# Two 1024x1024 layers of the last three token blocks, computed as seven products of quarters

## The chip, the core and the metric

The kernel runs on one core of a Trainium2 chip. The metric is the device time of one execution in microseconds (us); a smaller number is better. The engines of a core that matter here are TensorE (PE; its loads of stationary operands are listed apart as PEld), VectorE (DVE), ScalarE (ACT), GpSimd (POOL) and SyncE (SP, which only issues transfers here). POOL issues transfers too.

## What is computed

The input x is 4 x 1024 tokens of width 256. Three steps follow each other, each with a residual: a feed-forward network on normalised tokens (half of it is added), a long convolution over the sequence with a dense layer behind it, and the same feed-forward network again.

```python
h = silu(x @ w1.T * s1) * (x @ w2.T * s2)        # 256 -> 1024, twice
h = gelu(h @ h1.T * s_h1)                        # 1024 -> 1024, "layer 2"
h = gelu(h @ h2.T * s_h2)                        # 1024 -> 1024, "layer 3"
return h @ w3.T * s3                             # 1024 -> 256
```

The weights w1, w2, h1, h2 and w3 are drawn from -1, 0 and 1 (as float32 numbers).

## The kernel before

**Blocks.** The 4096 tokens are cut into eight blocks of 512 (`TB`). The outer loop (line 1029) runs over sixteen turns: f0 to f7 for the first network, g0 to g7 for the second. Between them the convolution ("mix") of each of the four sequences is worked in, and so is the preparation of its kernel.

**Precision.** The matmuls of the network take float32 operands in a reduced format, `float32r`. An activation is split into two such parts: the high part is a converting copy on ACT (line 367 or 379), the low part is the difference to it, made on DVE by `low_part` (line 285, its instruction has line 287). `linear` (line 340) adds up the product with both parts in one PSUM bank, so each weight tile is multiplied with two moving operands of 128x512. The weights are exact in one part, because they are small whole numbers; if they are not, the whole function is run a second time in plain float32 (`macaron_kernel`, line 1049), which does not happen with these inputs. `weight_checks` (line 455) finds that out: it loads each weight piece again in 44 pieces of 128x512 (tile `given`) and compares it on DVE with the resident copy.

**One turn.** `ffn` (line 352) makes 8 pairs of banks pa and pb (64 matmuls, with ACT's Silu and DVE's product behind them), then layer 2 with the resident `h1_sb` and layer 3 with `h2_sb` (8 banks of 16 matmuls each, line 374, with Gelu on ACT at line 377), then the last layer: `last_squares` (line 391, 2 banks of 16 matmuls of 512 columns) or, in turn g7, `last_tokens` (line 410), where activations are the stationary operand and w3 with 256 columns is the moving one (line 423). `xr` is the residual's input, `y` the result.

**Order of the work.** After each of the eight banks of a layer, `ffn` calls `ahead()` and `tick()`. `ahead` pushes `prepare` (line 956) of the next turn by a step: load of x, norm, transposition through a DRAM tile `moved` (POOL stores, line 317, and loads, line 325). `tick` (line 1007) hands out side work (`aside`: convolution and its kernel) for a budget of `STEP_WORK` = 2500, in which an operation on DVE counts its columns and `OP_WORK` = 130. When the side work pauses and more than eight entries are done, it takes a weight check instead. A scheduler of the framework then orders the instructions of each engine; each engine works its own list in order, and waits for others by semaphores. Tiles come from rings: `half` (19 buffers of 128x512), `ring` (15 operand tiles of two parts), and eight PSUM banks.

Of the kernel before, what the change touches and what calls it, by code (L numbers as in the profile page):

```python
# [2 lines left out]

# [8 lines left out]
F32 = mybir.dt.float32  # L12
# [3 lines left out]
ALU = mybir.AluOpType  # L16
# [16 lines left out]
N_WARM = 9  # L33


STEP_WORK, OP_WORK, MIN_WORK = 2500, 130, 300
PAUSE = "pause"
N_CHECKS = 44

EPS = 1e-5  # L40
INV_2PI = 1.0 / (2.0 * math.pi)
# [56 lines left out]
def macaron_layers(  # L98
# [20 lines left out]

    nc = tc.nc
    split = bad is not None
    wide = F32R if split else F32
# [3 lines left out]
    small = ctx.enter_context(tc.tile_pool(name="small", bufs=2))  # L128
    dram = ctx.enter_context(tc.tile_pool(name="dram", bufs=1, space=bass.MemoryType.DRAM))
    psum = ctx.enter_context(tc.tile_pool(name="psum", bufs=8, space=bass.MemoryType.PSUM))  # L130

    work_done = 0

# [18 lines left out]
    def half(name, *shape, dtype=F32):  # L152

        return work.tile([P, *(shape or (512,))], dtype, tag="half", name=name, bufs=19)
# [10 lines left out]
    make_identity(nc, ident)  # L165
    w1_sb = keep.tile([P, DC, HID], wide, name="w1_sb")
    w2_sb = keep.tile([P, DC, HID], wide, name="w2_sb")
    h1_sb = keep.tile([P, KH, HID], wide, name="h1_sb")
    h2_sb = keep.tile([P, KH, HID], wide, name="h2_sb")
    w3_sb = keep.tile([P, KH, D], wide, name="w3_sb")  # L170
    wt_sb = keep.tile([P, DC, D], F32, name="wt_sb")
    w3s_sb = keep.tile([P, D], F32, name="w3s_sb")
# [7 lines left out]

    moved = dram.tile([DC, P, JT, P], F32, name="moved")
    k_hat = dram.tile([2 + len(PAIRS), 2, P, 2, D], F32, name="k_hat")

    def column(i):
        return cst_sb[:, i : i + 1]
# [41 lines left out]
    x_first = work.tile([P, JT, D], F32, tag="xb", name="x_f0", bufs=3)  # L227
    for i, queue in ((0, nc.sync), (2, nc.scalar)):
        queue.dma_start(x_first[:, i : i + 2, :], tokens(x, 0, i, 2))
    eps = small.tile([P, 1], F32, name="eps", bufs=1)  # L230
    nc.vector.memset(eps, EPS)

    unused = small.tile([P, 1], F32, name="unused", bufs=1)
# [115 lines left out]
                    stop=(k == n - 1 and part == parts - 1),  # L349
                )  # L350

    def ffn(xt, src, dst, blk, name, tick, ahead, final):


        ha = []
        for m in range(KH):
            pa, pb = bank(f"pa_{name}_{m}"), bank(f"pb_{name}_{m}")
            linear(pa, w1_sb, m, xt)
            linear(pb, w2_sb, m, xt)
            g = half(f"g_{name}_{m}")  # L360
            t = ring(f"ha_{name}_{m}", parts, TB, dtype=wide)
            nc.scalar.activation(g, pa, AF.Silu, scale=sc_sb[:, 0, m : m + 1])
            nc.vector.scalar_tensor_tensor(  # L363
                g if split else t[:, 0, :], pb, sc_sb[:, 1, m : m + 1], g, ALU.mult, ALU.mult
            )
            if split:
                nc.scalar.copy(t[:, 0, :], g)
                low_part(t, g)
            ha.append(t)
        for layer, w in ((2, h1_sb), (3, h2_sb)):  # L370
            hb = []
            for m in range(KH):
                ps = bank(f"p{layer}_{name}_{m}")
                linear(ps, w, m, ha)
                t = ring(f"h{layer}_{name}_{m}", parts, TB, dtype=wide)
                g = half(f"g{layer}_{name}_{m}") if split else t[:, 0, :]
                nc.scalar.activation(g, ps, AF.Gelu, scale=sc_sb[:, layer, m : m + 1])  # L377
                if split:
                    nc.scalar.copy(t[:, 0, :], g)  # L379
                    low_part(t, g)  # L380
                hb.append(t)
                ahead()
                if layer == 2 or m < KH - 1:
                    tick()
            ha = hb
        ahead(last=True)
        if name == "f0":
            nc.scalar.mul(w3s_half, w3s_half, 0.5)
        (last_tokens if final else last_squares)(ha, src, dst, blk, name)

    def last_squares(ha, src, dst, blk, name):


        rest = []
        for k in range(DC):
            xr = half(f"xr_{name}_{k}", TB // SQ, SQ)
            for c in range(P // SQ):
                nc.sync.dma_start(xr[c * SQ : (c + 1) * SQ], in_squares(src, blk, k, c))
            rest.append(xr)
        for k in range(DC):  # L400
            ps = bank(f"po_{name}_{k}")
            linear(ps, w3_sb, k, ha)
            o, y = half(f"o_{name}_{k}"), half(f"y_{name}_{k}", TB // SQ, SQ)
            nc.scalar.activation(o, ps, AF.Identity, scale=w3s_half[:, k : k + 1])
            nc.vector.transpose(y, o.rearrange("p (n s) -> p n s", s=SQ))
            nc.gpsimd.tensor_tensor(y, rest[k], y, ALU.add)
            for c in range(P // SQ):
                stores.dma_start(in_squares(dst, blk, k, c), y[c * SQ : (c + 1) * SQ])

    def last_tokens(ha, src, dst, blk, name):  # L410

        rest = []
        for i in range(0, JT, 2):
            xr = half(f"xr_{name}_{i}", 2, D)
            nc.sync.dma_start(xr, tokens(src, blk, i, 2))
            rest.append(xr)

        def result(ps, i, n):

            for e in range(n):  # L420
                for k in range(KH):
                    for part in range(parts):
                        nc.tensor.matmul(  # L423
                            ps[:, e * D : (e + 1) * D],
                            ha[k][:, part, (i + e) * P : (i + e + 1) * P],
                            w3_sb[:, k, :],
                            start=(k == 0 and part == 0),
                            stop=(k == KH - 1 and part == parts - 1),
                        )

        def finish(ps, y, xr, i, n, add_on):
            nc.vector.scalar_tensor_tensor(
                y,
                ps.rearrange("p (e d) -> p e d", e=n),
                0.5,
                w3s_sb[:, None, :].to_broadcast([P, n, D]),
                ALU.mult,
                ALU.mult,
            )
            add_on.tensor_tensor(y, xr, y, ALU.add)  # L440
            nc.sync.dma_start(tokens(dst, blk, i, n), y)

        y = half(f"y_{name}_0", 2, D)
        ps = bank(f"po_{name}_0")
        result(ps, 0, 2)
        finish(ps, y, rest[0], 0, 2, nc.gpsimd)
        y = half(f"y_{name}_2", 2, D)
        for e in range(2):
            ps = bank(f"po_{name}_{2 + e}")
            result(ps, 2 + e, 1)  # L450
            finish(
                ps[:, 0:D], y[:, e : e + 1, :], rest[1][:, e : e + 1, :], 2 + e, 1, nc.vector
            )

    def weight_checks():

        todo = []
        for src, held in ((w1, w1_sb), (w2, w2_sb), (h1, h1_sb), (h2, h2_sb), (w3, w3_sb)):
            n_k, width = held.shape[1], held.shape[2]
            by = max(1, 512 // width)  # L460
            for k in range(0, n_k, by):
                for c in range(0, width, 512):
                    cols = slice(c, min(c + 512, width))
                    todo.append((rows(src)[:, k : k + by, cols], held[:, k : k + by, cols]))
        assert len(todo) == N_CHECKS

        def load(n):
            given = half(f"given_{n}", *todo[n][1].shape[1:])
            nc.sync.dma_start(given, todo[n][0])
            return given  # L470

# [2 lines left out]
        for n, (src, held) in enumerate(todo):  # L474
            given = following
            if n + 1 < len(todo):
                following = load(n + 1)
            stt(
                given,
                given,  # L480
                0.0,
                held.bitcast(F32),
                ALU.add,
                ALU.not_equal,
                accum_out=miss[:, n : n + 1],
            )
            yield
# [513 lines left out]

    aside = all_aside()
    checks = weight_checks() if split else iter(())
    ticks = 0
    allowed = 0

    def tick():

        nonlocal ticks, allowed, work_done
        ticks += 1  # L1010
        allowed = min(allowed, work_done) + STEP_WORK
        while work_done < allowed:
            at = work_done
            if next(aside, PAUSE) is PAUSE:
                if len(done) > 8 and allowed - work_done > OP_WORK + TB:
                    next(checks, None)
                break
            if work_done == at:
                work_done += MIN_WORK
# [9 lines left out]
    for n, (turn, blk) in enumerate(blocks):  # L1029
# [3 lines left out]
        def ahead(last=False):  # L1033
            for step in steps:
                if last:
                    done.append(("last layer", *blocks[n + 1][::-1]))
                next(step, None)

        src, dst = (x, x1) if turn == "f" else (x2, out)
        with tc.issue_after(last_split.ins) if n == 0 else nullcontext():  # L1040
            ffn(xt, src, dst, blk, f"{turn}{blk}", tick, ahead, n + 1 == len(blocks))
        done.append((turn, blk))
        xt = following
    for rest in (aside, checks):
        for _ in rest:
            pass


def macaron_kernel(tc: tile.TileContext, *args):
# [72 lines left out]
```

## Time and profile before

| what | value |
|---|---|
| median of 3 runs | 1405.83 us (1405.32 to 1405.91) |
| the profiled execution's own time | 1405.23 us |
| its span in the trace, first to last instruction | 1403.3 us |
| PE busy | 1393.0 us (99%) |
| PEld busy | 1161.4 us (83%) |
| DVE busy | 838.6 us (60%), 1614 instructions |
| ACT busy | 707.6 us (50%), 1070 instructions |
| POOL busy | 266.3 us (19%) |
| DMA | 101.27 MB, mean 72 GB/s |
| granted TensorE clock, mean | 0.999 of full speed |

A group row of the profile reads: line, engine, operation, out<-in, shapes, xcount, then busy time of the group, mean length of one instruction in ns, and the idle time of the engine just ahead of it. Matmuls overlap each other in the records, so their mean length is longer than the distance between two of them; distances are taken from the length of a run of them. A row of the stretches by window gives, for each engine, its busy time in the stretch and in brackets its instructions. Turn g5 runs from 1142 to 1236 us, g6 from 1236 to 1316 us, g7 from 1316 us to the end.

### The profile page before, as it was taken

The page shows a single profiled execution, that of the slowest core. Times are in us where ns is not written, and L with a number is a line of the kernel's source. Part 1 is how long each engine was busy: PE and PEld are TensorE (multiplying, and loading weights), DVE is VectorE, ACT ScalarE, POOL GpSimd, SP SyncE. Part 2 cuts the span into 40 slices and gives each one's busy share as a digit, 9 for nine tenths or more (in the row PEclk, how much of TensorE's full clock was granted, in tenths as well). Part 3 has the DMA queues.
Part 4 walks back from the last instruction along what each step waited for, and adds up shares of the span by engine and source line. Part 5 has one row for each costly group of instructions (what it writes and reads, how often), then busy time and mean ns, then how long its engine had stood idle before and what let it go on. Part 6 is the DMA issues. An engine that isn't in the chain of part 4 may idle for free.

```text
span 1403.3 us, 17882 instructions
## 1 busy us (share of the span) xinstructions
PE 1393.0 (99%) x6492; PEld 1161.4 (83%) x6492; DVE 838.6 (60%) x1614; ACT 707.6 (50%) x1070; POOL 266.3 (19%) x398
## 2 busy tenths in 40 slices
PE   8999999999999999999999999999999999999998
PEld 7888888888888888888888888888888888888887
DVE  6896567755547774387773568753566762542412
ACT  5986579644546344354352454533545342553532
POOL 4321012211312120320113201213112121121200
PEclk9999999999999999999999999999999999999999
DMA  9410101112231322422213404132223122511000
GB/s 355 117 20 26 35 16 46 30 48 77 67 96 30 113 71 73 136 60 84 61 53 113 113 31 138 20 97 74 86 70 82 43 63 98 135 22 39 15 16 19
DMA packets 111139, 101.27 MB, mean 72 GB/s; under 512 B 72304, under 2 KB 82544, under 8 KB 111040
## 3 DMA queue, kind: packets, MB, share of 16 engines
q1 hardware_dynamic: 93248, 55.37, 14.6%
q0 software_dynamic: 17520, 44.39, 11.1%
q8 instruction: 53, 0.87, 0.3%
q14 instruction: 46, 0.38, 0.1%
q10 hardware_dynamic: 272, 0.26, 0.1%
HBM read 76.91 MB, written 23.07 MB: 71 GB/s over the span
## 4 chain that ended last, share of the span: by engine, by line
PE 99%; DMA 1%; POOL 0%; DVE 0%; issue 0%; POOLq 0%
PE p_f L344 33%; PE p_g L344 33%; PE po_f L344 4%; PE pa_g L344 4%; PE pb_g L344 4%; PE pa_f L344 4%; PE pb_f L344 4%; PE po_g L344 4%; PE pi L905 2%; PE pf_m L727 2%; PE pw L930 2%; PE pk L654 1%; PE po_g L423 1%; DMA w_sb<-in_w_dram 1%; PE pf_k L727 0%; POOL w_sb L238 0%
## 5 line engine op out<-in xcount | busy, mean ns | idle before, releaser
L287 DVE TENSOR_TENSOR h_g<-g_g,h_g 128x512 fp32r<-128x512 f32 x128 | 88.6, 692 | 249.6 <-ACT h_g L379 249.3
L344 PE MATMUL p_f<-h_f,h_sb 128*128 128x512 f32 x1024 | 237.1, 391 | 0.0
L344 PE MATMUL p_g<-ha_g,h_sb 128*128 128x512 f32 x1024 | 236.2, 390 | 0.0
L344 PE MATMUL p_f<-ha_f,h_sb 128*128 128x512 f32 x1024 | 235.3, 390 | 0.0
L344 PE MATMUL p_g<-h_g,h_sb 128*128 128x512 f32 x1024 | 235.2, 390 | 0.0
L377 ACT ACTIVATE g_g<-p_g,sc_sb 128x512 f32<-128x512 f32 x128 | 88.2, 689 | 278.9 <-PE p_g L344 276.5
L344 PEld LDWEIGHTS p_g<-ha_g,h_sb 128*128 128x128 f32 x1024 | 192.1, 188 | 39.8
L344 PEld LDWEIGHTS p_g<-h_g,h_sb 128*128 128x128 f32 x1024 | 192.1, 188 | 39.8
L344 PEld LDWEIGHTS p_f<-h_f,h_sb 128*128 128x128 f32 x1024 | 191.8, 188 | 40.1 <-DVE h_f L287 0.3
L344 PEld LDWEIGHTS p_f<-ha_f,h_sb 128*128 128x128 f32 x1024 | 191.9, 188 | 39.8
L377 ACT ACTIVATE g_f<-p_f,sc_sb 128x512 f32<-128x512 f32 x128 | 87.7, 689 | 190.0 <-PE p_f L344 189.6
L287 DVE TENSOR_TENSOR h_f<-g_f,h_f 128x512 fp32r<-128x512 f32 x128 | 87.8, 690 | 149.0 <-ACT h_f L379 148.5
L317 POOL DMA_DIRECT2D moved<-sq_g x64 | 34.9, 552 | 330.3 <-DVE sq_g L140 290.7
L379 ACT CAST h_g<-g_g 128x512 fp32r<-128x512 f32 x128 | 79.3, 620 | 4.0
L379 ACT CAST h_f<-g_f 128x512 fp32r<-128x512 f32 x128 | 78.3, 618 | 2.9
L377 ACT ACT_TABLE_LOAD x51 | 65.4, 1283 | 26.0 <-PE p_f L344 14.3
L344 PE MATMUL pa_f<-xt_f,w_sb 128*128 128x512 f32 x256 | 69.0, 390 | 1.1 <-DVE xt_f L299 0.7
L344 PE MATMUL pb_f<-xt_f,w_sb 128*128 128x512 f32 x256 | 68.8, 389 | 0.0
L344 PE MATMUL pa_g<-xt_g,w_sb 128*128 128x512 f32 x256 | 68.4, 389 | 0.0
L344 PE MATMUL pb_g<-xt_g,w_sb 128*128 128x512 f32 x256 | 68.4, 389 | 0.0
L363 DVE SCALAR_TENSOR_TENSOR g_g<-pb_g,sc_sb,g_g 128x512 f32<-128x512 f32 x64 | 47.9, 749 | 31.5 <-PE pb_g L344 19.7
L317 POOL DMA_DIRECT2D moved<-sq_f x56 | 30.8, 556 | 181.2 <-DVE sq_f L140 181.2
(234 smaller groups left out, 1844.4 us busy)
## 6 DMA issues: line engine op xcount, KB each, us to landing
h_sb<-in_h_dram POOLq DMA_DIRECT2D x8, 1024.0 KB, 15.0
given<-in_h_dram SPq DMA_DIRECT2D x32, 256.0 KB, 3.6
kr<-k_hat SPq DMA_DIRECT2D x20, 256.0 KB, 2.6
ki<-k_hat SPq DMA_DIRECT2D x20, 256.0 KB, 2.8
xr_f<-in_x_dram SPq DMA_DIRECT2D x64, 64.0 KB, 2.4
x<-y_f POOLq DMA_DIRECT2D x64, 64.0 KB, 2.2
xm<-x SPq DMA_DIRECT2D x8, 512.0 KB, 3.7
m_m<-in_cosm_dram SPq DMA_DIRECT2D x16, 256.0 KB, 5.2
```

The costliest lines, as they stand in the source:

```text
L287: return nc.vector.tensor_tensor(t[:, 1, :], src, t[:, 0, :].bitcast(F32), ALU.subtract)
L317: stores.dma_start(moved[k].rearrange("(c r) a q -> a r c q", r=SQ)[a], sq[a * SQ : (a + 1) * SQ].rearrange("r c j s -> r c (j s)"),)
L344: nc.tensor.matmul(ps, w[:, k, m * P : (m + 1) * P], acts[k][:, part, :], start=(k == 0 and part == 0), stop=(k == n - 1 and part == parts ...
L363: nc.vector.scalar_tensor_tensor(g if split else t[:, 0, :], pb, sc_sb[:, 1, m : m + 1], g, ALU.mult, ALU.mult)
L377: nc.scalar.activation(g, ps, AF.Gelu, scale=sc_sb[:, layer, m : m + 1])
L379: nc.scalar.copy(t[:, 0, :], g)
L423: nc.tensor.matmul(ps[:, e * D : (e + 1) * D], ha[k][:, part, (i + e) * P : (i + e + 1) * P], w3_sb[:, k, :], start=(k == 0 and part == 0) ...
L654: nc.tensor.matmul(pk[0:NA, at + i, :, :].rearrange("p h b -> p (h b)"), a[:, i].rearrange("p a b -> p (a b)"), qd[d1 // per_tile][:, at + ...
L727: nc.tensor.matmul(ps[e][:, part, :], m[:, e, part, :], rows_of(q + JQ * e), start=True, stop=True)
L905: nc.tensor.matmul(banks[dc][e][:, q * P : (q + 1) * P], vs[q + JQ * e][:, part, dc * P : (dc + 1) * P], m[:, e, part, :], start=(part == ...
L930: nc.tensor.matmul(ps[:, e * D : (e + 1) * D], yts[dc][j // JQ][:, (j % JQ + e) * P : (j % JQ + e + 1) * P], wt_sb[:, dc, :], start=(dc == 0),
```

## The change

The diff acts on turns g5, g6 and g7 only (`N_BY_SUMS` = 3), apart from the budget and what prepares the weights.

- Layers 2 and 3 of these turns are computed by `winograd`. Weights are cut into 2x2 quarters of 512x512, activations into 2x2 quarters of 512 features x 256 tokens. Seven products of quarters take the place of eight; each has 32 matmuls of 256 columns (`product`). The sums of activations are made on DVE (`less`, `plus`) with copies out of PSUM on ACT (`kept`); each product's moving operand is split into two parts anew (`operand`). A layer so has 14 conversions and 14 low parts, 8 differences, 6 sums from PSUM, 6 copies out of PSUM and 16 activations of 128x256.
- `weight_sums` makes the sums of weight quarters beforehand on DVE and ACT from the resident weights, and stores seven quarter matrices for each layer (1 MB each) in DRAM, with 56 stores from POOL. It takes the fillers' turn ahead of the weight checks.
- Before g5 the room of `h1_sb` and `h2_sb` is given back. In it lie four slots of 1 MB for quarters, and six tiles (`raw`) for unsplit activations. SP loads the next quarter into a slot after each product (`load_slot`).
- The checks of h1 and h2 no longer compare with the resident copy but with the sign of the loaded piece itself, which is one more activation on ACT.
- The last layer splits its input by the same `operand`, and in g5 and g6 runs in two halves of 256 tokens (64 matmuls of 256 columns for 32 of 512). In g7 tokens 256 to 511 come first.
- From g0 on the budget of `tick` is 3000, and the convolution has to be complete before g5.

```diff
+    def operand(quarter, name):
+        ops = []
+        for p, src in enumerate(quarter):
+            t = ring(f"{name}_{p}", parts, TB, dtype=wide)
+            nc.scalar.copy(t[:, 0, :], src)
+            low_part(t, src)
+            ops.append(t)
+        return ops
...
+    def product(banks, weights, ops, step, first=True):
+        for p, ps in enumerate(banks):
+            for e in range(2):
+                m = 2 * p + e
+                for c in range(QK):
+                    for part in range(parts):
+                        nc.tensor.matmul(
+                            ps[:, e * QT : (e + 1) * QT],
+                            weights[:, c, m * P : (m + 1) * P],
+                            ops[c // 2][:, part, c % 2 * QT : (c % 2 + 1) * QT],
...
+            step()
...
+    def winograd(raw, layer, name, step):
+        pa = pair(f"p{layer}a_{name}")
+        out = [raw_tile(f"h{layer}_{name}_{p}") for p in range(KH // 2)]
...
+        def times(banks, ops, first):
+            product(banks, slots.pop(0), ops, step, first)
+            load_slot()
...
+        b11 = operand(of(0, 0), named("b11"))
+        t1 = less(of(0, 1), of(0, 0), named("t1"))
+        t1_ops = operand(t1, named("t1s"))
+        times(pa, b11, True)
+        p1 = kept(pa, named("p1"))
+        t2 = less(of(1, 1), t1, named("t2"))
+        t2_ops = operand(t2, named("t2s"))
+        pd = pair(f"p{layer}d_{name}")
+        times(pd, t1_ops, True)
+        p5 = kept(pd, named("p5"))
+        b21 = operand(of(1, 0), named("b21"))
+        times(pa, t2_ops, False)
+        u2 = kept(pa, named("u2"))
+        t3 = less(of(1, 1), of(0, 1), named("t3"))
+        t3_ops = operand(t3, named("t3s"))
+        pe = pair(f"p{layer}e_{name}")
+        times(pe, b21, True)
+        activated(out, 0, 0, plus(p1, pe), layer)
+        b22 = operand(of(1, 1), named("b22"))
+        times(pa, t3_ops, False)
+        activated(out, 1, 1, plus(p5, pa), layer)
+        t4 = less(t2, of(1, 0), named("t4"))
+        t4_ops = operand(t4, named("t4s"))
+        times(pd, b22, False)
+        activated(out, 0, 1, plus(u2, pd), layer)
+        times(pa, t4_ops, False)
+        activated(out, 1, 0, pa, layer)
+        return out
...
+    def load_slot():
+        if coming:
+            src, name = coming.pop(0)
+            t = late.tile([P, QK, QW], F32R, tag="slot", name=name, bufs=N_SLOTS)
+            nc.sync.dma_start(t.bitcast(F32), src)
+            slots.append(t)
...
+                tt(s1, a[1, 0], a[1, 1], ALU.add)
+                nc.scalar.mul(minus, a[1, 1], -1.0)
+                tt(s3, a[0, 0], a[1, 0], ALU.subtract)
+                yield
+                tt(s2, s1, a[0, 0], ALU.subtract)
+                tt(s4, a[0, 1], s2, ALU.subtract)
...
+                    stores.dma_start(quarters[layer][i][:, c, :], t)
...
+        n_t = TB // n_parts
+        for n in reversed(range(n_parts)):
+            for o, ps in enumerate(banks):
+                order = sorted(range(KH), key=lambda k: k < QK) if n else range(KH)
...
+            if held is None:
+                other = half(f"sign_{n}", *given.shape[1:])
+                nc.scalar.activation(other, given, AF.Sign)
...
-        allowed = min(allowed, work_done) + STEP_WORK
+        allowed = min(allowed, work_done) + (
+            STEP_WORK_2 if ("f", n_blocks - 1) in done else STEP_WORK
+        )
...
-                    next(checks, None)
+                    next(fillers, None)
...
+        by_sums = split and n >= len(blocks) - N_BY_SUMS
+        if by_sums and not slots:
+            assert ("m", B - 1) in done
+            for _ in sums_of_weights:
+                pass
+            wide_pool.__exit__(None, None, None)
...
+            for _ in range(N_SLOTS):
+                load_slot()
```

## The prediction

> **What bounds the kernel now.** I read the page first: busy time by engine, then the chain that ended last. Two kinds of line carry the answer.
>
> ```profile
> span 1403.3 us, 17882 instructions
> PE 1393.0 (99%) x6492; PEld 1161.4 (83%) x6492; DVE 838.6 (60%) x1614; ACT 707.6 (50%) x1070; POOL 266.3 (19%) x398
> PE 99%; DMA 1%; POOL 0%; DVE 0%; issue 0%; POOLq 0%
> ```
>
> TensorE is the path: 10 us of the span are not PE. So the change is worth what it takes from PE, less the waits that it makes. Next the chain in order of time and the timeline, for the distance between two matmuls.
>
> ```profile
> 1077.15 58.03 PE p_g L344 x256
> 1391.14 5.57 PEld L423 LDWEIGHTS po_g<-w_sb,h_g 128*128 128x128 f32 x46 [0.20 <-DVE h_g L287]
> L423 PEld LDWEIGHTS po_g<-w_sb,h_g 128*128 128x128 f32 x64 | 7.9, 191 | 0.3 <-DVE h_g L287 0.2
> ```
>
> A matmul of 512 columns takes 58.03 / 256 = 0.2267 us. The trace has the new shape too: turn g7's last layer has 256 columns. The 46 loads of stationary operands start within 5.57 - 0.19 = 5.38 us; over 45 distances that is 0.1195 us each. The record of one load is 191 ns long, so loads overlap. Half the columns cost 53% of the time.
>
> Then the groups of DVE and ACT by form, the stretches by window, and the transfers.
>
> ```profile
> L287 DVE TENSOR_TENSOR h_g<-g_g,h_g 128x512 fp32r<-128x512 f32 x128 | 88.6, 692 | 249.6 <-ACT h_g L379 249.3
> L140 DVE SCALAR_TENSOR_TENSOR given<-given,h_sb 128x512 f32<-128x512 f32 x32 | 21.9, 683 | 9.7 <-DMA given<-in_h_dram 9.7
> L379 ACT CAST h_g<-g_g 128x512 fp32r<-128x512 f32 x128 | 79.3, 620 | 4.0
> L731 ACT COPY f_m<-pf_m 128x512 f32<-128x512 f32 x16 | 9.4, 586 | 8.9 <-PE pf_m L727 8.7
> L800 ACT ACTIVATE k_minus<-x_k 128x256 f32<-128x256 f32 x3 | 1.2, 410 | 0.0
> 1236.00:1316.00 80.00, 80.00 (x355) 65.97 (x354) 26.68 (x41) 34.73 (x52) 13.10 (x21) 1.00 0.13 27
> 1316.00:1403.00 87.00, 80.92 (x387) 67.97 (x385) 25.09 (x38) 34.03 (x51) 7.77 (x10) 0.98 0.07 20
> 15.00:20.00 5.00, 5.00 (x24) 4.14 (x23) 4.17 (x7) 3.76 (x8) 1.14 (x2) 1.00 1.12 420
> 18.31 0.56 POOL L216 DMA_DIRECT2D x_f<-in_x_dram  x1 [1.89 <-DMA h_sb<-in_h_dram]
> 20.79 0.55 POOL L216 DMA_DIRECT2D x_f<-in_x_dram  x1 [1.92 <-DMA h_sb<-in_h_dram]
> ```
>
> DVE has 53 us free in g6, which the change means to use. The last two lines show resident weights, 1 MB each, landing one behind another 2.48 us apart (420 GB/s in that stretch).
>
> **TensorE.** A layer of 128 matmuls is 29.02 us; 224 of 256 columns are 224 x 0.1195 = 26.77 us. That is 2.25 us less, six times: -13.5. The halved last layers of g5 and g6 are 64 x 0.1195 = 7.65 for 32 x 0.2267 = 7.25: +0.8 together. g7's count stays. PE: **-12.7 us**.
>
> A rule speaks against this. The Trainium skill, "TensorE: Matmul & The Clock Gate", sections LDWEIGHTS and weight-path perf modes, has a load take its columns / 1.2 ns, 107 ns here, without a fast form for float32. Laid end to end with 107 ns of streaming (its back-to-back section) that is 213 ns per matmul: 47.8 us per layer, +113 us. If the 191 ns record were the pace it would be 42.8 us, +83. The row has both in 119.5 ns at this very shape, so I take the row.
>
> **DVE and ACT in the three turns.** Per turn, low parts go from 24 to 36, differences 16 and PSUM sums 12 are new: 40 x 0.69 = 27.6 us. With g6's 26.7 this makes 54 us in a turn of 14.5 + 53.5 + 7.65 = 75.7. ACT: 12 more conversions (7.4), 12 copies (7.0), 32 half activations (13.1) for 16 whole ones at 0.689 (-11.0): +16.5, so 51. Checks come on top (0.683 and an 0.08 accumulator read on DVE, about 0.63 for the sign on ACT): by the built order of instructions 15 stand in g5, 6 in g6. DVE in g5 is then 54 + 11.6 = 66 us, 87%; ACT 61, 80%. On the mean it fits, but queues are in order. A check waits for its sign, that for its transfer, and behind the check stand low parts for which PE waits.
>
> So I walked the built order by these durations, by hand, from the start of g5's first product (3.82 us each). One case in full: product 6 runs from 19.1 to 23.0. DVE finishes the second sum of p5 at 19.8 (product 5 ended at 19.1), a low part of b22 at 20.5, a check at 21.3, both differences t4 at 22.7, the first sum of u2 at 23.3, the first low part of t4 at 24.0. Product 7 needs that at 23.1: 0.9 late. In the same way layer 3's product 2 is 1.0 late, product 3 0.4, product 7 1.7, and the last layer 1.6, its second half of operands standing behind two checks and a Gelu of the last product. Sum in g5: **+5.6**, between 0 (the mean fits) and 12. In g6 six checks and the next turn's norm end within 0.2 us of what PE needs: I take **+1** (0 to 3). In g7 each low part is 0.8 us or more ahead: 0. The operations from PSUM are costed by like rows; hand-overs of 0.03 us, not counted, are what could add to this, 0 to 8 us over the six layers.
>
> **What runs earlier.** Sums of weights: 32 x 0.685 = 22 us of DVE, 5 of ACT, 56 stores at 0.55 = 31 us of POOL, and their 14.7 MB. They take the place of checks from turn f5 on, where POOL is at 14 to 22% and DVE at 49 to 79%, and lie beside PE: 0. If that cover were gone, it would be 22. Behind a store in POOL's queue stand `moved` and `xf`, which PE needs only a turn's start later. The budget of 3000 allows 4.7 operations of 642 for a tick, 3.2 us, with the tile's own low part 3.9 us for a bank of 3.63; before it was 3.4. While mixing goes at full rate DVE slips 0.3 us per bank, and a late low part hurts only at a layer's end, where the last tile has 14 x 0.2267 = 3.2 us. I take **+1** (0 to 3). The table loads of ACT stay about equal in number: 0. None of this can gain, as PE has no wait before g5 that could be shortened.
>
> **Quarters.** 42 loads of 1 MB on SP. Each waits for a product's end and is needed three products, 11.5 us, later. Behind it on SP stand checks' loads and residuals; SP's read of the checks' result waits in g6 for a DVE copy that my walk puts 43 us into the two layers; the quarter behind it is asked for at 45. The trace has no such load on SP; the nearest row is POOL's: 2.48 us each, with a check's 256 KB 3.1, under 3.82. The Trainium skill, "DMA: Bandwidth & Descriptors", measured transfers, gives 6.15 us for a single 1 MB. Taken one at a time, ten refills in a turn would end at 3.8 + 61.5 = 65.3 for a product due at 49.7: 15.6 late per turn, +47 us. The row shows them pipelined, so I take 0; late it gets above 4.6 us each.
>
> **Sum.** 1405.2 (the profiled execution) - 12.7 + 5.6 + 1 + 1 = 1400.1. That execution is 0.6 below the median of the runs, so **1400.7**.
>
> **Rivals.**
> - *The chain of vector work paces every product (slower).* Each product opens with a low part that stands behind a sum which waits for the product before. If g6 and g7 wait like g5, 5.6 a turn, it is 1405.8 - 12.7 + 16.8 + 1 = 1410.9. It decides from 12.7 / 42 = 0.3 us of wait a product. For it: 87% in g5, in-order queues handing to each other several times in each product. Against: g7 has no checks and DVE is at 70%. Chance 0.17.
> - *The waits eat most of the gain.* 10 to 15 us of waits instead of 7.6: 1403 to 1408.6, middle 1405. Chance 0.15.
> - *No waits to speak of.* PE runs ahead as today: 1405.8 - 12.7 + 1 = 1394.1. For it: means leave room everywhere. Chance 0.10.
> - *It doesn't do what it says*: quarters land late (1441) or loads of operands pace PE (near 1480). Against: both rows above. Chance 0.04.
> - *As summed*, 1395.5 to 1403: chance 0.54.
>
> A measurement of this kernel can tell about 0.2%, 2.8 us, from no change. Faster by more: 0.54 + 0.10 = 0.64; within: 0.15; slower: 0.17 + 0.04 = 0.21. The range goes from 1394.5, just above the case without waits, to 1411, the first rival's value, which leaves out about 0.1 on the slow side and 0.08 on the fast one. The likeliest case alone: 1395.5 to 1403.
>
> **What would show it.** Products of 32 matmuls 3.82 us long, where nothing is awaited; PE idle (now near none) of about 5 us in g5 against DVE low parts, 1 in g6, none in g7; DVE busy near 66 us in g5; quarters landing in under 8 us with no PE wait on a transfer; turns before g5 as long as today. I'm wrong if g7 has waits of microseconds (then hand-overs, not checks, set the pace), if a product without waits isn't 3.82 us, if PE waits for a quarter, or if f5 to g4 grow.

## The result, and the profile after

The changed kernel takes **1399.49 us** in the median of 6 runs (1397.57 to 1401.98), the kernel before 1405.72 (1405.32 to 1405.91, 6 runs): ratio 0.9956, 95% interval 0.9946 to 0.9967. Its runs lie 4.4 us apart, those of before 0.6. The profiled execution took 1398.44 us, 1 us less than the median, with a span of 1396.7.

First the page of the changed kernel: span, busy time by engine, shares of the chain that ended last, and the two transfers that matter (count, KB each, median us from issue to landing).

```profile
span 1396.7 us, 19695 instructions
PE 1384.2 (99%) x7132; PEld 1182.6 (85%) x7132; DVE 932.8 (67%) x1766; ACT 766.8 (55%) x1227; POOL 297.0 (21%) x454
PE 93%; DVE 3%; DMA 2%; ACT 1%; issue 0%; POOL 0%; SPq 0%; DVEq 0%; POOLq 0%; ACTq 0%
w<-q SPq DMA_DIRECT2D x42, 1024.0 KB, 6.1
given<-in_h_dram SPq DMA_DIRECT2D x32, 256.0 KB, 5.0
```

TensorE is still the path, but its share of the chain fell from 99% to 93%; DVE and ACT now have shares, and that of DMA went from 1% to 2%. So somewhere PE waits, and transfers may stand behind that. Next the timeline of PE in g7, where nothing is awaited (start, length, operation; the length of a group includes the overlap of its last matmul).

```profile
1328.36 4.00 PE L484 MATMUL p2a_g<-b_g,w 128*128 128x256 f32 x32
1332.19 4.00 PE L484 MATMUL p2d_g<-t1s_g,w 128*128 128x256 f32 x32
...
1378.27 4.00 PE L484 MATMUL p3a_g<-t4s_g,w 128*128 128x256 f32 x32
1382.11 3.16 PE L658 MATMUL po_g<-w_sb,hl_g 128*128 128x256 f32 x25
```

Fourteen products take 1382.11 - 1328.36 = 53.75 us, 3.84 us each. In g5 the same view has gaps, in brackets with what ended them:

```profile
1192.75 2.90 PE L484 MATMUL p2d_g<-b_g,w 128*128 128x256 f32 x22 [0.31 <-DVE b_g L309]
1204.22 3.86 PE L484 MATMUL p3d_g<-t1s_g,w 128*128 128x256 f32 x30 [0.33 <-DVE t1s_g L309]
1227.71 0.50 PE L630 MATMUL po_g<-hl_g,w_sb 128*128 128x256 f32 x2 [0.23 <-ACT hl_g L465]
1228.43 0.97 PE L630 MATMUL po_g<-hl_g,w_sb 128*128 128x256 f32 x6 [0.23 <-DVE hl_g L309]
1230.25 0.51 PE L630 MATMUL po_g<-hl_g,w_sb 128*128 128x256 f32 x2 [0.84 <-ACT hl_g L465]
```

A wait costs more than its bracket: around the second line the next product starts at 1207.92, 4.53 us after this one's first matmul at 1203.39, so 0.69 us is lost for a bracket of 0.33. Therefore I add up by stages, from the first matmul of each:

| stage (first matmul to first matmul), us | before | after |
|---|---|---|
| first turn to g4's end, incl. all mixing | 8.85 to 1142.27: 1133.42 | 9.25 to 1157.38: 1148.13 |
| g5 | 93.88 (14.1 of mixing in it) | 80.18 |
| g6 | 80.15 | 76.26 |
| g7 to its last layer | 72.53 | 68.29 |
| last layer to the span's end | 14.47 | 14.59 |

The mixing that stood in g5 has moved to g4, so the first two rows are read together: 1227.30 before, 1228.31 after, 1.0 us lost, where g6 and g7 gain 3.9 and 4.2. So g5's own saving is gone, and more. The question for the experiments is what took it.

The trace names a suspect: a check's load. Timeline of all engines around the second of the gaps above (other lines left out):

```profile
1202.20 0.64 ACT L714 ACTIVATE sign<-given 128x512 f32<-128x512 f32 x1 [1.08 <-DMA given<-in_h_dram]
1202.73 1.12 ACT L465 CAST t1s_g<-t_g 128x512 fp32r<-128x512 f32 x2
1202.86 0.69 DVE L156 SCALAR_TENSOR_TENSOR given<-given,sign 128x512 f32<-128x512 f32 x1 [0.18 <-ACT sign L714]
...
1203.48 1.29 DVE L309 TENSOR_TENSOR t1s_g<-t_g,t1s_g 128x512 fp32r<-128x512 f32 x2
```

The check's Sign stood at the head of ScalarE's queue for 1.08 us until its load landed; behind it stood the conversion of t1, behind that VectorE's low part, and for that PE waited. The list of waits in g5 (1157 to 1240 us) says how often (us in all, times, longest):

```profile
ACT sign L714 <- DMA given<-in_h_dram: 5.2, 5, 1.4
```

and the group of `given` in the same stretch how long its loads take:

```profile
DMA to landing us min/median/max: 2.7/6.8/8.3
```

Five such waits. A load is issued one check ahead, and a check comes about once a product, 3.84 us; the load lands after 6.8. No other instruction of g5 waits for these loads in that list.

The first of the five gaps is of another kind: no Sign near it waits for a load. VectorE's queue has the second sum of product 5, which needs that product's end, ahead of a low part that product 6 needs:

```profile
1191.40 0.69 DVE L536 TENSOR_TENSOR p_g<-p2a_g,p_g 128x512 f32<-128x512 f32 x1 [0.38 <-PE p2a_g L484]
1192.01 0.68 DVE L309 TENSOR_TENSOR b_g<-g_g,b_g 128x512 fp32r<-128x512 f32 x1
```

That order costs product 6 about 0.8 us. Every kernel below is ordered anew when it is built, and an order can change along with the thing that is tested.

### The profile page after: what moved, and what is told of

It reads as the page before. It is cut to its first block, busy times and chain, and to the rows that moved or that the text cites. A ratio compares the mean times of both kernels' runs of the same rounds, so it can differ in the third digit from the quotient of the medians.

```text
span 1396.7 us, 19695 instructions
## 1 busy us (share of the span) xinstructions
PE 1384.2 (99%) x7132; PEld 1182.6 (85%) x7132; DVE 932.8 (67%) x1766; ACT 766.8 (55%) x1227; POOL 297.0 (21%) x454
## 4 chain that ended last, share of the span: by engine, by line
PE 93%; DVE 3%; DMA 2%; ACT 1%; issue 0%; POOL 0%; SPq 0%; DVEq 0%; POOLq 0%; ACTq 0%
PE p_f L366 31%; PE p_g L366 19%; PE pa_f L366 4%; PE pa_g L366 4%; PE pb_f L366 4%; PE pb_g L366 4%; PE po_f L630 4%; PE po_g L630 4%; PE p2a_g L484 3%; PE p3a_g L484 3%; PE pi L1144 2%; PE pw L1169 2%; PE pf_m L966 2%; PE p2d_g L484 1%; PE p3d_g L484 1%; PE pk L893 1%
## 5 line engine op out<-in xcount | busy, mean ns | idle before, releaser
L418 ACT ACTIVATE g_g<-p_g,sc_sb 128x512 f32<-128x512 f32 x80 | 55.2, 690 | 174.6 <-PE p_g L366 165.0
L366 PE MATMUL p_g<-ha_g,h_sb 128*128 128x512 f32 x640 | 148.1, 391 | 0.0
L366 PE MATMUL p_g<-h_g,h_sb 128*128 128x512 f32 x640 | 147.9, 391 | 0.1
L366 PEld LDWEIGHTS p_g<-h_g,h_sb 128*128 128x128 f32 x640 | 120.0, 188 | 25.4 <-ACT h_g L420 0.5
L366 PEld LDWEIGHTS p_g<-ha_g,h_sb 128*128 128x128 f32 x640 | 120.0, 188 | 24.7
L309 DVE TENSOR_TENSOR h_g<-g_g,h_g 128x512 fp32r<-128x512 f32 x80 | 55.2, 690 | 111.8 <-ACT h_g L420 111.3
L392 DVE SCALAR_TENSOR_TENSOR g_f<-pb_f,sc_sb,g_f 128x512 f32<-128x512 f32 x64 | 47.3, 746 | 23.0 <-PE pb_f L366 15.9
```

What stands on the lines that cost most here:

```text
L309: return nc.vector.tensor_tensor(t[:, 1, :], src, t[:, 0, :].bitcast(F32), ALU.subtract)
L366: nc.tensor.matmul(ps, w[:, k, m * P : (m + 1) * P], acts[k][:, part, :], start=(k == 0 and part == 0), stop=(k == n - 1 and part == parts ...
L392: nc.vector.scalar_tensor_tensor(g if split else t[:, 0, :], pb, sc_sb[:, 1, m : m + 1], g, ALU.mult, ALU.mult)
```

## Experiments

Theory W: the loss is the wait of ScalarE's in-order queue for loads that land late, because since the change they share SyncE's queue with a 1 MB quarter per product. Rivals: V, the checks' own time on the two engines; B, preparation in earlier turns; D, quarters that come late. Twelve kernels; "late" below means from g5 on.

### Without the late checks

```
         for n, (src, held) in enumerate(todo):
+            if slots:
+                break
...
```

(the 21 checks from g5 on, with their loads, are left out)

> The changed kernel, but the 21 weight checks that it runs in g5 and g6 are left out (their counts stay zero), with their loads and Sign steps; the final sum of counts stays. Theory (products of quarters wait only where the in-order VectorE and ScalarE queues hold a check ahead of the step that the product needs): g5 loses its waits, its 14 products take about 53.8 us instead of 55.6 and its last layer about 7.8 instead of 10.0, so about 4 us less than the changed kernel: 1395.5 us (1394.5 to 1396.5), and the scatter between runs shrinks from 4.4 us towards the 0.6 us of the kernel before. Rival A (the splits and differences that the products need are themselves too slow in a turn that also prepares the next): waits stay, 1399. Rival B (a large part of the loss lies in the earlier turns): 1398 or more.

Measured: **1393.33 us** (1393.07 to 1393.77), ratio 0.9910 (0.9896 to 0.9925). More than the 4 us expected, and below the range: 6.2 us less than the changed kernel's median. Its profiled execution is 4.7 below that of the changed kernel, of which g5 has 3.94 (76.24 us for 80.18). Its g5 also holds two small matmuls of the checks' final count, 0.3 us, which the changed kernel has in g6; so g5's waits are 4.2 us. The scatter falls to 0.7 us. So the late checks and their loads are the loss and the scatter. That excludes this run's rival A (the splits and differences themselves are too slow), and B for all but a small rest; it doesn't yet tell W from V.

### Checks only in the second layer

```
-                        if layer == 2 or at < 14:
-                            tick()
+                        if layer == 2 or at < 14:
+                            tick(layer == 2)
```

(a tick with a false argument draws no check)

> The changed kernel with all 44 checks, but in g5, g6 and g7 a check may start only behind a product of the second layer, not of the third: 8 in g5, 8 in g6, 5 in g7 instead of 15, 6 and 0. Theory: the waits of g5's third and last layers (0.3 us and some 2.2 us in the profile) go, those of its second layer stay and g6 and g7 may get 0.3 us each: 1396.5 us (1395.5 to 1398). Rival (the last layer of g5 waits for its own splits, not for checks): 1399 to 1400. Rival (each check costs its own time wherever it is): no change, 1399.5.

Measured: 1399.16 us (1397.86 to 1404.92): the time of the changed kernel, with more scatter. The expectation missed. g5 is shorter (78.98 us for 80.18), but g6 went from 76.26 to 78.40 and g7 by 0.4: eight checks now stand in g6 and five in g7, and the waits moved with them.

### Preparation only

```
-N_BY_SUMS = 3
+N_BY_SUMS = 0
```

(the sums of weights are formed and stored, and not used)

> The changed kernel with no turn by sums: all layers as eight-term products of 512 columns, while the sums of weights are still formed and stored, the tick budget is 3000 and the checks compare with Sign. Theory (preparation costs a little in g0 to g4): 1406.5 us (1405.7 to 1407.5). Rival A (preparation wholly hidden): 1405.7, as the kernel before. Rival B (preparation takes 2 us or more, so that the products' own gain is larger than seen): 1408 or more.

Measured: 1407.20 us (1406.40 to 1407.79, 11 runs), ratio 1.0010 (1.0001 to 1.0019): 1.5 us over before, inside the theory's range. The stages of its trace, though, put only 0.3 us of it into the turns (its last layer begins at 1389.15 for 1388.83). The rest lies behind the last addition: from its end, 1397.74 + 0.42, to the end of the span at 1404.8 it is 6.6 us, for 5.4 before. What that is stays open; the changed kernel has 5.8 there and the one without late checks 5.3, so it doesn't come with the preparation as such.

### Two turns instead of three

```
-N_BY_SUMS = 3
+N_BY_SUMS = 2
```

> The changed kernel with two turns by sums (g6, g7) instead of three. Theory (g5's own gain is eaten by its waits for checks: 55.6 + 10.0 us for its products and last layer against 58.0 + 7.3 us of an ordinary turn, and the checks behind ordinary layers find room): as fast as three turns, 1399.3 us (1398.3 to 1400.5). Rival (each turn by sums is worth the same third of what was gained): 1401.5 to 1402. Rival (all of a turn's 4.1 us of TensorE time comes back, the waits move to g6): 1403.5.

Measured: **1397.60 us** (1397.25 to 1397.74), ratio 0.9941 (0.9928 to 0.9954): two turns by sums are *faster* than three, by 1.9 us in the medians, more than the expectation allowed, and the scatter is 0.5. Of the 21 late checks 15 now run in an ordinary g5 (79.78 us), and nearly all of their loads land soon, as no quarter is on the queue yet. The landing times of `given` in the same stretch of this kernel (1157 to 1240 us):

```profile
DMA to landing us min/median/max: 2.5/2.5/10.1
```

A median of 2.5 us for 6.8, for the same 256 KB on the same queue. The 10.1 is the one load issued behind quarters, at 1238.09. So the lateness comes from the quarters.

### Loads three checks ahead, and two

```
-            given = half(f"given_{n}", ...)
+            given = half(f"given_{n}", ...) if late is None else late.tile(..., tag="given", bufs=4)
...
+            while n + len(loaded) + 1 < len(todo) and len(loaded) < (1 if late is None else 3):
+                loaded.append(load(n + len(loaded) + 1))
```

(for two ahead: 3 tiles, and 2 in the place of 3)

> The changed kernel in full, all 44 checks where they were, but from g5 on the loads of the weights to be compared go to four tiles of their own and are issued three checks ahead instead of one. Theory W (the loss is the wait of Sign, at the head of ScalarE's in-order queue, for a load that was issued one check earlier and lands some 6.8 us later in these turns: 5.2 us of such waits in g5): these waits go, g5 takes some 77 us instead of 80.2, and the whole 1395 us (1393.5 to 1396.5), with little scatter. Theory V (the loss is the check's own time on the two engines, 0.63 us on ScalarE and 0.77 us on VectorE, ahead of the product's steps): no change, 1399 us.

> As the kernel with loads three checks ahead, but two ahead (three tiles). Theory W (the loss is the time by which a load lands after the engine wants it: landing 6.8 us, against some 3.9 us of one check's lead): two checks' lead is 7 to 8 us at one check a product, just enough in the median and not for the slowest (8 to 9 us): 1396 to 1397 us, with more scatter than the 1 us of three ahead. Rival (the gain came from giving the loads tiles of their own, whatever the lead): the same as three ahead, 1395.7.

Measured: three ahead **1395.70 us** (1395.01 to 1395.97), ratio 0.9928 (0.9916 to 0.9941); two ahead 1397.37 (1396.91 to 1399.07), ratio 0.9948 (0.9934 to 0.9961). Every check still runs, at almost the same places. By lead the medians are 1399.5, 1397.4, 1395.7, and the scatter 4.4, 2.2, 1.0. Between two and three only the lead (and with it the number of tiles) differs. From one to two the loads get tiles of their own as well, and the two causes aren't separated there. In the profiled executions g5 is the same with two and three ahead (77.16 us); two ahead loses time in g6 (78.28 for 77.10), where a comparison on VectorE waits 1.4 us and a Sign 0.8 for a load. With three ahead the landing time is unchanged, but no wait of ScalarE's Sign for a load is left. The landing times of `given` in g5:

```profile
DMA to landing us min/median/max: 3.4/6.7/9.2
```

That is theory W. V, which wanted 1399, is out as the main cause. One part of the gain isn't W's, though: this kernel has product 6's low part (1188.18) ahead of both sums of product 5, so the first gap's 0.8 us went with the new order. What is left over the kernel without late checks is 2.4 us in the medians. By stages 0.9 of it is in g5, whose last layer is 1.1 longer (8.74 us for 7.68), and 1.1 in g6. The PE timeline has a wait in each:

```profile
1226.27 8.18 PE L630 MATMUL po_g<-hl_g,w_sb 128*128 128x256 f32 x62 [0.22 <-DVE hl_g L309]
1257.35 3.99 PE L484 MATMUL p2a_g<-t2s_g,w 128*128 128x256 f32 x31 [0.47 <-DVE t2s_g L309]
```

Ahead of the low part that the second line waits for, three checks run in VectorE's queue from 1254.71 to 1256.61. That is what V describes, and it is small.

### Checks without loads

```
+            if late is not None:
+                return fake[0].rearrange(...)
...
-                given,
+                result,
                 given,
```

(`fake` is a constant tile, `result` a tile of its own for the outcome)

> The changed kernel, but the 21 checks from g5 on load nothing: Sign and the comparison run on a constant tile, so these weights go unchecked, while each check keeps its 0.63 us on ScalarE and 0.77 us on VectorE at its place. Theory W (waits for loads are the loss): 1394 us (1393 to 1395.5), near the 1393.3 us of the kernel without these checks. Theory V (own time is the loss): 1398 to 1400.

Measured: 3930.9 us, which says nothing of the question: the constant differs from the last weights compared, so the flag was set and the program's second branch, the whole computation in float32, ran as well. That was a mistake in the edit. The first pass in its trace can still be read by stages: g5 77.26 us, g6 77.33, g7 to its last layer 68.29, against 77.16, 77.10, 68.29 with the loads three ahead. No product in the three turns waited; g5's last layer and g6's first layer did:

```profile
1226.54 8.17 PE L630 MATMUL po_g<-hl_g,w_sb 128*128 128x256 f32 x62 [0.23 <-DVE hl_g L309]
1235.58 1.10 PE L366 MATMUL pa_g<-xt_g,w_sb 128*128 128x512 f32 x3 [0.64 <-DVE xt_g L309]
```

So loading nothing is worth no more than loading early. The last layer of g5 takes 8.73 us for 7.68, as with the loads three ahead: about 1 of g5's 3.94 us is the checks' own steps. The other 2.9 went with the loads, but the new order is in that (the low part of product 6 stands ahead of product 5's sums here too): about 0.8 for the order leaves about 2.1 for the late loads. g6 gets 1.1 us longer than in the changed kernel, in part by this wait: now that g5 ends sooner, what feeds g6 is late next.

### Loads without checks

```
+            if late is not None:
+                yield
+                continue
             if held is None:
```

> The changed kernel, but from g5 on the weights to be compared are loaded as before and neither Sign nor the comparison runs on them, so they go unchecked. Theory W and theory V: no engine waits for the loads, as fast as without the checks, 1393.3 us (1393 to 1394). Rival D (the 5.5 MB of these loads slow the quarters on the same queue, and products wait for quarters): 1395 or more, with a wait of the weight loads for the transfer of a quarter in the trace.

Measured: 1398.56 us (1397.55 to 1401.30), ratio 0.9953 (0.9940 to 0.9965). Both theories missed: I wrote that nothing waits for a load that nobody reads. No product waits for a quarter, so rival D is not what happens. Two other things do. The list of waits in g5 has two on the loads all the same:

```profile
ACT u_g L503 <- DMA given<-in_h_dram: 1.5, 1, 1.5
ACT p_g L503 <- DMA given<-in_h_dram: 1.4, 1, 1.4
```

These are copies of a product's sums out of PSUM. I take it that they were given the tile of a load still on its way, into which they must not write before it has landed. And the order of VectorE's queue is another one here: it has the sum of product 4 ahead of the difference t3, so that t3 waits for product 4 and product 5 for t3:

```profile
1185.72 0.69 DVE L536 TENSOR_TENSOR p_g<-p2e_g,p_g 128x512 f32<-128x512 f32 x1 [5.97 <-PE p2e_g L484]
1186.33 1.28 DVE L474 TENSOR_TENSOR t_g<-g_g,g_g 128x512 f32<-128x512 f32 x2
...
1188.98 3.25 PE L484 MATMUL p2a_g<-t3s_g,w 128*128 128x256 f32 x25 [0.76 <-DVE t3s_g L309]
```

In the changed kernel the differences start at 1182.81, before that sum at 1185.53. So this run is confounded, and it teaches another point: a late load stops whoever gets its tile, not only who reads it. The runs with loads in tiles of their own rule out this wait too. In the changed kernel's g5 the list of waits has none of this kind, so there it can't have been much; how much it gave of the first 2.1 us, from one check ahead to two, isn't separated.

### Loads on GpSimd's queue

```
-            nc.sync.dma_start(given, todo[n][0])
+            (nc.sync if late is None else stores).dma_start(given, todo[n][0])
```

> The changed kernel in full, with the loads of the weights to be compared issued from GpSimd's queue from g5 on, away from SyncE's, on which each follows a 1 MB quarter. Theory W with the place on the queue as the reason for the late landing: the loads land in 4 us or less instead of 6.8, the waits of Sign shrink by half or more, 1396 us (1394.5 to 1397.5). If the transfers only share the 16 engines with the quarters: landing stays near 6 us and so does the time, 1398.5 to 1400; GpSimd's stores that wait for VectorE may also hold the loads back, and then it is slower than the changed kernel.

Measured: **1402.15 us** (1399.98 to 1403.76), ratio 0.9975 (0.9966 to 0.9984), slower than the changed kernel. The median landing is 4.8 us, between the 2.5 without quarters and the 6.8 behind them, but GpSimd's queue holds the loads back, behind stores that wait for VectorE and for tiles to come free (`given` alone waits 17.3 us in g5 for its tiles). GpSimd's timeline shows the last loads bunched at the end of g5:

```profile
1200.28 0.54 POOL L703 DMA_DIRECT2D given<-in_h_dram  x1 [3.31 <-DVE given L156]
1212.27 2.21 POOL L339 DMA_DIRECT2D moved<-sq_g  x4 [11.46 <-DVE sq_g L156]
1214.47 0.56 POOL L703 DMA_DIRECT2D given<-in_h_dram  x1
...
1219.60 0.56 POOL L703 DMA_DIRECT2D given<-in_h_dram  x1
```

The load of 1214.47 took 8.2 us to land and that of 1219.60 took 7.8, which is 1222.7 and 1227.4. Just then the signs start, and the last layer waits (timeline of ACT and PE):

```profile
1222.72 0.63 ACT L714 ACTIVATE sign<-given 128x512 f32<-128x512 f32 x1 [1.85 <-DMA given<-in_h_dram]
...
1227.48 0.63 ACT L714 ACTIVATE sign<-given 128x512 f32<-128x512 f32 x1 [2.29 <-issue]
...
1230.19 0.53 PE L630 MATMUL po_g<-hl_g,w_sb 128*128 128x256 f32 x2 [4.24 <-ACT hl_g L465]
```

It is W again, on a worse queue. The second wait has "issue" beside it, as no releaser was found; the landing time gives it. Whether a load is late because it stands behind a quarter on one queue, or because the two are on their way at once, this run doesn't separate.

### Two tiles for quarters

```
-N_SLOTS = 4
+N_SLOTS = 2
```

(on the kernel without the late checks)

> The kernel without the late checks (1393.3 us), with two tiles for quarters instead of four: a quarter is asked for when the product before the last one ends, so it has one product's 3.84 us instead of three products' 11.5 us to land. Theory (a quarter lands in 5.1 us in the median, one at a time, as no other is on its way): from the third product of g5 on each product waits some 1.3 to 2 us, 40 times: 1445 to 1475 us, with TensorE waiting for the transfer of w. Rival (the landing time is mostly queueing behind other quarters, and a lone quarter comes at the 2.5 us pitch of the first weight loads): no wait, 1393 to 1396.

Measured: 1424.81 us (1423.58 and 1426.05), 31.5 over its base (1393.33), 0.79 us for each of 40 products: the theory's direction, and 20 us less than its range. PE now waits for quarters (its timeline):

```profile
1208.16 4.07 PE L484 MATMUL p3d_g<-t1s_g,w 128*128 128x256 f32 x32 [1.32 <-DMA w<-q]
1229.08 5.57 PE L484 MATMUL p3d_g<-b_g,w 128*128 128x256 f32 x32 [1.86 <-DMA w<-q]
```

One quarter at a time lands after 4.8 us (median, 1157 to 1240 us), 1.0 over a product. With four tiles no product ever waited for a quarter.

### Better versions

(the kernel with loads three ahead, and checks only in the second layer)

> The changed kernel in full with the loads three checks ahead in tiles of their own, as in the run that took 1395.7 us, and from g5 on a check only behind a product of the second layer: 8 in g5, 8 in g6, 5 in g7. That run still lost 0.9 us in g5 and 1.1 us in g6: the transposed input of g6 was late, as the tile that it is loaded to came free late, and the first products of g6 had four checks ahead of a split. Theory (what is left comes from the checks' tiles and steps in the crowded places): g6's late input goes, 1394.5 us (1393.8 to 1395.3). Rival (own time of a check counts wherever it stands): no change, 1395.5 to 1396; with six more checks behind g6's and g7's first layers perhaps more.

Measured: 1395.17 us (1394.00 to 1396.60), ratio 0.9923 (0.9909 to 0.9936). Not told apart from the same kernel with checks in both layers (1395.70). In its profile g5 is at 75.94 us, without loss, and g6 at 78.48: once more the loss moved with the checks. And once more loads come late: the last checks compare with weights that are still resident, need no Sign, and wait on VectorE itself, 2.66 us at 1280.56 and 4.06 us at 1289.43. Their loads went out at 1271.60 and 1279.24 and took 8.9 and 10.2 us, longer than the lead that they had there. In the same stretch two products of g6 wait for low parts of VectorE, at 1283.30 and 1292.60.

```
-STEP_WORK, STEP_WORK_2, OP_WORK, MIN_WORK = 2500, 3000, 130, 300
+STEP_WORK, STEP_WORK_2, OP_WORK, MIN_WORK = 2500, 3500, 130, 300
```

(on the kernel with loads three ahead)

> The kernel with all checks and their loads three ahead (1395.7 us), with the tick budget after the last f turn at 3500 instead of 3000: 30 checks run before g5 instead of 23, 14 in g5, none in g6. Theory (the earlier turns have room on VectorE and ScalarE, and what is left of the loss is the checks' own time in turns by sums): g6 gets its 1.1 us back, g5 keeps some 0.5 to 1 us, g0 to g4 stay as they are: 1394.6 us (1393.9 to 1395.4). Rival (a larger budget crowds g0 to g4 as well, as the 3000 already did by part of the 1.5 us of the preparation): 1396 to 1398.

Measured: **1394.83 us** (1394.15 to 1395.43), ratio 0.9925 (0.9911 to 0.9938): a kernel with every check and the lowest median of them, 4.7 us below the changed kernel, though not told apart from 1395.17. By its trace 33 of the 44 checks are done before g5, for 23 in the changed kernel, and the other 11 stand in g5. g5 takes 76.24 us, as without late checks; PE has no wait of 0.2 us or more from g4 to g7. g5's start, 1157.23, is where it was: the larger budget costs the earlier turns nothing that shows.

## Why the prediction was right, and where its reasons were not

The time was predicted at 1400.7 and is 1399.49. By the steps:

- **TensorE, -12.7: right, 0.7 too much.** The row's 0.1195 us per matmul of 256 columns came out as 3.84 / 32 = 0.1200, so fourteen products take 53.75 us for 53.54, 0.6 us over the three turns. The halved last layers take 7.68 us for 7.25 (predicted 7.65). Without late checks the three turns are 3.6, 4.2 and 4.2 us shorter than as ordinary turns, 12.0 in all (79.79, 80.15 and 72.53 against 76.24, 75.96 and 68.29, the last up to the last layer). The rule that the prediction weighed against it, loads of operands at 107 ns laid end to end with their matmuls, would have made a product 6.8 us; the trace decided rightly.
- **Waits, +5.6 in g5 and +1 in g6: near in size, but half of them have another cause.** The late checks cost 6.2 us in the medians (1399.49 - 1393.33). In the profiled execution the waits are 4.2 us, all of them in g5 (80.18 - 76.24, and the 0.3 of the final count's matmuls that g5 holds without late checks). g6 has no wait of PE at all, for +1 predicted. The walk made them all out of the engines' own work. Part of that is real: about 1 us of the checks' own steps in the last layer, and the 0.8 at product 6, where the walk's own chain has the low part of b22 end at 20.5, 1.4 us after product 6 began, and doesn't count it. The other half, about 2.1 us, is late loads. The walk had a check wait for its sign and that for its transfer, and never asked when the transfer lands.

Moreover the walk charged each operation its record's length, and operations in a row overlap. With loads three ahead, four VectorE operations follow each other like this in its timeline:

```profile
1264.64 0.69 DVE L309 TENSOR_TENSOR b_g<-g_g,b_g 128x512 fp32r<-128x512 f32 x1
1265.24 0.69 DVE L536 TENSOR_TENSOR p_g<-p2e_g,p_g 128x512 f32<-128x512 f32 x1
1265.84 0.69 DVE L309 TENSOR_TENSOR b_g<-g_g,b_g 128x512 fp32r<-128x512 f32 x1
1266.44 0.69 DVE L474 TENSOR_TENSOR t_g<-t_g,g_g 128x512 f32<-128x512 f32 x1
```

Each is 0.69 us long and starts 0.60 after the one before, so a chain of them was put some 15% too long. In the case that the prediction gives in full, seven operations from 19.1 on end at 23.4 with these distances, not at 24.0, and two thirds of its 0.9 us are gone. g5's VectorE busy time was put at 66 us, and a window of 80 us over g5 of the changed kernel has 59.62:

```profile
1157.50:1237.50 80.00, 77.84 (x577) 73.77 (x576) 59.62 (x110) 56.16 (x107) 12.74 (x20) 1.00 0.81 283
```

(columns: window, its length, then busy us and count of PE, PEld, DVE, ACT, POOL, then PE's clock, the DMA share and GB/s)

So the step that failed is "walked the built order by these durations": too long for the own work, and with nothing in it for landing. Of the five places named, layer 3's product 2 (there by a late load) and the last layer are in the trace, product 7 of layer 2 is product 6 there, and layer 3's products 3 and 7 started on time. That the sum fitted is luck: one error made it too large and the other too small.

- **Earlier turns, +1: right in the sum.** The profile of the changed kernel has 1.0 us there. Preparation alone measured +1.5, but with 0.3 of it in the turns and the rest behind the last addition, so what makes the 1.0 is not shown. (g5 starts at 1157.38; before, g5's end less an ordinary turn is 1236.15 - 79.79 = 1156.36.) The profiled executions add up: -12.0 + 4.2 + 1.0 + 0.1 from the last layer on is -6.7, and the spans differ by 6.6.
- **Quarters, 0: right.** No product waited for one, and they land in 6.1 us of the 11.5 that they have. The Trainium skill's "DMA: Bandwidth & Descriptors" (measured transfers) gives 6.15 us for a single 1 MB, issued from GpSimd. Taken one at a time here, from SP, it was 4.8; with two tiles, so that each had one product's time, that cost 31.5 us. But the step looked only at whether quarters are late, not at whom they make late. The prediction named the checks' loads behind the quarters on SP, and then priced only the quarters.
- **Rivals.** That vector work paces every product fell: g7 runs at 3.84 us a product with no wait. That nothing waits fell for the changed kernel. It came close to true in the kernel with early loads and a budget of 3500: 1394.83, and 1394.1 was put for it. Two values of the rivals are slips in sums: 15 us of waits give 1408.1, not 1408.6, and loads of operands at 191 or 213 ns give about 1489 or 1519, not 1480. Neither bore on the result.

## What to carry to other kernels

When a change puts large transfers on a queue, list every small load already on it and compare its lead (how long before its use it is issued) with the landing time it will now have; raising the lead from one check to three, in tiles of their own, was worth 3.8 us here, more than half of what the change itself brought; some of that may be the order that came with it. A consumer at the head of an in-order queue passes such a wait on to everything behind it, and a tile from a common ring passes it on to work that has nothing to do with the load. And read a chain of operations by the distance between starts, not by the length of the records.

## What the runs showed of the hardware

- The same 256 KB load landed in 2.5 us (median) with the queue to itself and in 6.8 with a 1 MB load per 3.84 us beside it; a lone 1 MB landed in 4.8 us.
- Kernels in which work waits on such loads scattered more from run to run: 4.4 us with the loads one check ahead, 7.1 with the checks in one layer, 3.8 on GpSimd's queue, 2.2 and 2.6 in the two with early loads where a check still waited for one in g6. Without late checks, with two turns by sums, three ahead and with the budget of 3500 it was 0.5 to 1.3 us. Each is the spread of four to ten runs.
- VectorE operations of 0.69 us in a row start 0.60 us apart; five conversions in a row on ScalarE, 0.61 us each alone, took 2.69 us in all, 0.52 apart.
